# A pre-norm decoder layer: two quarters' attention outputs summed in PSUM, cross scores negated in the keys' norms, and the first cross rows requested beside their norms

## The chip, the core and the metric

The kernel runs on one core of one Trainium2 chip. The metric is device time in microseconds, the median over several runs. Engines are called TensorE (PE in the profile, with its weight loads as PEld), VectorE (DVE), ScalarE (ACT), GpSimd (POOL) and SyncE (SP). SP and POOL also issue DMAs, each from a queue of its own that is worked through in order.

## The reference

The layer takes `x` and a context `ctx_2048`, both (4, 512, 512) in float32, and adds three branches to `x`, each on layer-normalized rows.

```
q = (x @ Wq + bq).reshape(B, T, 128, 16)      # 16 heads, k and v likewise
y = softmax(q^T k / sqrt(128)) v              # attention over the 128 features of a head
x = x + y @ Wo + bo
# cross attention: norm(x) is (B, 512, 512); the 512 rows are split into 8 heads of 64
qk = einsum('bhdq,bhdl->bhql', norm(x), ctx) / sqrt(64)
x = x + gamma * einsum('bhql,bhdl->bhdq', softmax(qk), ctx)
# feed-forward with ternary weights, hidden size 1365
x = x + (silu(norm(x) w1q^T) * (norm(x) w3q^T)) w2q^T
```

`w1q`, `w3q`, `w2q` are weights rounded to -1, 0 or 1 times their mean absolute value.

## The kernel before

**Phase A (0 to about 285 us).** For each of four batches the normalized rows become a Gram matrix (`gram_upper`, `gram_rest`); `keys_of` multiplies it by the key weights, `scores` forms the scores and their softmax, and the result is turned and kept in device memory (`kept_e`). The steps run over four quarters j of the heads and, inside, over the four batches b. Beside it `kept_weights` splits the value and output weights into three parts (h, l, d) and stores them; `scale_steps` sums the absolute values of the feed-forward weights. Matrix products are made from halves in a 32-bit format that TensorE runs at one pass: an `h` and an `l` product into one PSUM bank, a `d` product into another, added by `total` (line 378).

**Side work.** Such work beside the main products is written as Python generators. A `Side` holds one: at each `tick` of the main products it takes as many steps as keep it in proportion (n steps in `of` ticks). `products` ticks three times for each pair of output blocks, six times in all (`PRODUCT = 6`): after the second k of the h and l matmuls, after their evictions, and at the end of the pair. A `yield` in a generator ends a step.

**The attention outputs (about 285 to 825 us).** A loop over b and j makes, for each quarter, `values_out` (the products pu, of the rows with the output weights: u), and `values_of` (the products pm, of u with the value weights: ms). Between pu and pm u has to be split in three parts: ScalarE makes uh (line 197), VectorE ul and ud (198, 199). `output(b, j, ...)` is one plain float32 matmul for each of four row groups (po, line 570; 512 columns, shown as two records) and an addition on VectorE into the accumulators `accs` (line 571); it is called after the *next* quarter's `values_out`, so that it lies between that quarter's pu and pm. After the last quarter the accumulators are stored as `x_a`. All weights come in through `weights`, 12 tiles of 256 KB for each product from a ring of 20, and the turned softmax by `turned_kept` (eT, a ring of two); both are issued on SP, where the order is the program's (`manual_schedule` for SP and GpSimd). On the other engines the order is made by a planner when the program is built, from its own costs and the program's order.

**Cross attention.** For batch b - 1 it starts in the outputs of batch b. `row_norms` (line 686) takes mean and variance of each accumulator row, a step for each row group, and turns them on their side through a small store (`norm_a`) and two loads (`norms`). `cross` (704) then works in 16 rounds of two softmax blocks: `fetch` loads 64 rows of `x_a` (xd) and of the context (kd), twice over the partitions; `split` makes q and the two halves of the keys, with the norms as ScalarE's and VectorE's operands; `softmax_rows` makes the scores (xs), their row maxima (line 755), a factor on these (756), the exponential (761) and the division by its sum; `transpose_rows` turns the result (xp). A round of four is a chunk: the context rows (`keys`, turned to `vals`, matmuls vt), the matmuls xo (794), and the addition of `gamma` times the result to the rows of `x_a` (`xc`, line 802), which is stored as `x_c`. All these DMAs are issued on GpSimd. `settle` (613) multiplies a column of a loaded tile by a one made from a fresh eviction on VectorE, so that VectorE, in its place in the order, takes the wait for the load.

The steps of `row_norms` and the first of `cross` (`AHEAD` of them, 17) are ticked as `aside` in the first 12 ticks after the output of a batch is finished (18 in batch 1); `begin_cross` then hands the 56 that remain to `side`, over 48 ticks (42 in batch 1). So the end of one batch's cross attention and the beginning of the next lie in the same product. Batch 3's cross attention runs beside the feed-forward of the first batches.

**Feed-forward (from about 825 us).** Products h (line 1183) and y (1221), with weights kept on the chip.

Five small things set the order where the change touches it. The eT ring has two tiles, the ms ring four and the accumulators' eight. PSUM has eight banks, shared by all products. The pool `c_x` has a single tile for each of xd, kd and `late` (keys and xc), so each of these loads waits until the tile before it has been read.

Of the kernel before, what the change touches and what calls it, by code (L numbers as in the profile page):

```python
# [11 lines left out]
F32 = mybir.dt.float32  # L12
# [7 lines left out]
P = 128  # L20
# [21 lines left out]
def decoder_layer_kernel(  # L42
# [161 lines left out]
    def load(dst, src):  # L204
        nc.sync.dma_start(dst, src)
        return dst
# [89 lines left out]
    def kept_weights(pool):  # L296

        def items():
            for j in range(HG):
                for k in range(KC):  # L300
                    yield "o", j, k, None
                for k in CHUNKS:
                    yield "v", j, k, None

        sources = {}

        def bring(n, j, k):
            if n == "o":
                t = pool.tile([P, GW], F32, tag="raw_v", bufs=4, name=f"o_raw_{j}_{k}")
                load(t, by_group(wo[j * T : (j + 1) * T, :], k))  # L310
                return t
            if k == KC - 1:
                sources[j] = raw_of("v", j, pool, load, 4)
            return sources[j][1](k)

        coming = []
        for item in itertools.chain(items(), [None, None]):
            if item is not None:
                coming.append((item[:3], bring(*item[:3])))
                if len(coming) < 3:  # L320
                    continue
            (n, j, k), t = coming.pop(0)
            gate = gates[0]
            if n == "v":
                fold(k, t, sources[j][0], gate)
            tri = Tri(
                *(pool.tile([P, GW], F32R, tag="made", bufs=4, name=f"{n}{p}_{j}_{k}") for p in "hl"),
                t.bitcast(F32R),
            )
            halves_of_weight(tri.h, tri.l, t, gate)  # L330
            third_of_weight(tri)
# [5 lines left out]
    KEPT_STEPS = 2 * 2 * HG * KC  # L337

    def weights(n, b, j, wp):

# [223 lines left out]
    def turned_kept(b, j):  # L564
        return load(ep.tile([P, GW], F32, tag="e", name=f"eT_{b}_{j}"), kept_e[b, j])

    def output(b, j, eT, ms, accs):
        for g in range(NG):
            po = bank(f"po_{b}_{j}_{g}")
            nc.tensor.matmul(po, lhsT=eT[:, ts(g, DH)], rhs=ms[g], start=True, stop=True)  # L570
            nc.vector.scalar_tensor_tensor(accs[g], po, S * S, accs[g], ALU.mult, ALU.add)
            if j == HG - 1:
                nc.gpsimd.dma_start(by_group(x_a[b], g), accs[g])
# [104 lines left out]


    xscale = 1.0 / math.sqrt(XD)  # L680
    CROSS_STEPS = 3 * 4 * NC + 14
    NORM_STEPS = 2 * NG + 3
    AHEAD = NORM_STEPS + 6
    norms = {}

    def row_norms(b, accs):


        mv = small.tile([P, NG, 2], F32, tag="mvc", bufs=2, name=f"mv_c_{b}")
        for g in range(NG):  # L690
            yield
            moments(mv[:, g, :], accs[g], f"c_{b}_{g}")
        rstd = rstd_of(mv, f"c_{b}")
        mean, var = (mv[:, :, i : i + 1].rearrange("p c s -> p (c s)") for i in range(2))
        nc.vector.tensor_scalar(mean, mean, -1.0, None, ALU.mult)
        nc.vector.tensor_copy(var, rstd)
        nc.gpsimd.dma_start(norm_a[b].rearrange("(p g) s -> p g s", g=NG), mv)
        norms[b] = small.tile([P, 2 * NC, 2], F32, tag="norms", bufs=2, name=f"norms_{b}")
        for half in (slice(0, XD), slice(XD, P)):
            nc.gpsimd.dma_start(norms[b][half], norm_a[b].rearrange("(n p) s -> p n s", p=XD))  # L700
        for _ in range(NG + 3):
            yield

    def cross(b, cx, cin, cpp, cpt):

# [6 lines left out]
        def load(dst, src):  # L712
            nc.gpsimd.dma_start(dst, src)  # L713
            return dst

        def late(name, src):
            return load(cx.tile([P, T], F32, tag="late", name=f"{name}_{b}"), src)

        def fetch(n):

# [22 lines left out]
        def softmax_rows(n, h):  # L743
# [8 lines left out]
                scs.append(sc)  # L752
            nmax = small.tile([P, 2], F32, tag="xnmax", name=f"xnmax_{b}_{n}_{h}")
            for i in range(2):
                nc.vector.reduce_max(nmax[:, i : i + 1], scs[i], axis=AX.X)  # L755
            nc.vector.tensor_scalar(nmax, nmax, -xscale, None, ALU.mult)
            den = small.tile([P, 2], F32, tag="xden", name=f"xden_{b}_{n}_{h}")
            ps = []
            for i in range(2):
                p = cpp.tile([P, T], F32, tag="p", name=f"p_{b}_{n}_{h}_{i}")  # L760
                nc.scalar.activation(  # L761
                    p,
                    scs[i],
                    AF.Exp,
                    bias=nmax[:, i : i + 1],
                    scale=xscale,
                    accum_out=den[:, i : i + 1],
                )
                ps.append(p)
# [13 lines left out]

        def turn_values(c):
            vals[c] = cin.tile([P, NC, P], F32, tag="vals", bufs=1, name=f"vals_{b}_{c}")
            transpose_blocks(vals[c], rows[c], f"vt_{b}_{c}", True)

        def weigh_values(c, xc):
            pt = [pts.pop(2 * c + j) for j in range(2)]
# [12 lines left out]
            nc.vector.scalar_tensor_tensor(y, po, gam, xc, ALU.mult, ALU.add)  # L802
            return lambda: load(x_c[b][ts(c, P), :], y)

        raw, halves, vals, pts, rows, ps = {}, {}, {}, {}, {}, {}
        fetch(0)
        yield
        yield
        settle(norms[b][:, 0, :])
        yield  # L810
        split(0)
        yield
        fetch(1)
# [4 lines left out]
        for i in range(len(order) + 3):  # L818
            c, phase = divmod(i, 4)
            if phase == 3 and c < NC:  # L820
                rows[c] = late(f"keys_{c}", kv[b][ts(c, P), :])
            if i < len(order):
                ps[order[i]] = softmax_rows(*order[i])
            if i < len(order):
                yield
            if phase == 2 and c > 0:
                store = weigh_values(c - 1, rows.pop(c - 1))
                yield
            if 2 <= i < len(order) + 2:
                n, h = order[i - 2]  # L830
                transpose_rows(n, h, ps.pop((n, h)))
            if i % 2 == 0 and i // 2 + 1 < heads:
                split(i // 2 + 1)
            if i % 2 == 0 and i // 2 + 2 < heads:
                fetch(i // 2 + 2)
            if phase == 2 and c > 0:
                store()
            if i < len(order) + 2:
                yield
            if phase == 0 and c > 0:  # L840
                turn_values(c - 1)
            if phase == 1 and c > 0:
                rows[c - 1] = late(f"xc_{c - 1}", x_a[b][ts(c - 1, P), :])
            if i < len(order) + 2:
                yield

# [189 lines left out]
    PRODUCT = 6  # L1036
    TICKS = 2 * HG * PRODUCT
    quant, aside, side = Side(), Side(), Side()
    waiting, accs = None, None

    def tick():
        quant.tick()
# [18 lines left out]

    for b in range(B):
        for j in range(HG):
            if b == 0 and j == 0:
                wo_tiles = weights("o", b, j, wp)
                accs = accumulators(0)
                load(bo_bc, bo.to_broadcast([P, D]))
            else:
                if j == HG - 1 and b + 1 < B:
                    next_accs = accumulators(b + 1)  # L1070
                wo_tiles = weights("o", b, j, wp)
            u3 = values_out(b, j, x3, wo_tiles, tick if b + j > 0 else turning())
            if b == 0 and j == 0:
                quant = Side(each(ternary_steps, stp), 2 * PIECES, B * TICKS - 2 * PRODUCT)
            if waiting:
                output(*waiting)
            if j == 0 and b > 0:
                aside.rest()
                crossing = itertools.chain(row_norms(b - 1, accs), cross(b - 1, *cpool))
                aside = Side(itertools.islice(crossing, AHEAD), AHEAD, (3 if b == 1 else 2) * PRODUCT)  # L1080
                accs = next_accs
            if j == 1 and b > 1:
                begin_cross(TICKS)
            if j == HG - 2:
# [30 lines left out]
    rows_next = rows_f(1)  # L1115
    for _ in ffn_0:
        pass
    output(*waiting)
    for _ in row_norms(B - 1, waiting[4]):
        pass  # L1120
    apools.close()

# [21 lines left out]
    crossing = itertools.chain([None] * 11, cross(B - 1, *cpool))  # L1144
    before = Side(itertools.chain(side.steps, [None] * LEFT), LEFT, 9)
    aside = Side(itertools.islice(crossing, AHEAD), AHEAD, 9)

# [9 lines left out]
        if at > 9:  # L1157
            last.tick()

    last = Side(crossing, CROSS_STEPS - 6, 2 * (NHC + NC) + 2 - 9)  # L1160
# [118 lines left out]
```

## Time and profile before

| | us |
|---|---|
| median of 3 runs | 1145.51 |
| lowest and highest | 1143.5, 1145.91 |
| the profiled execution | 1143.08 |
| span of that execution, first to last instruction | 1141.3 |
| TensorE busy | 1124.5 |
| VectorE busy | 808.1 |
| ScalarE busy | 562.4 |
| additions into acc, L571, 64 of 685 ns | 42.9 |
| output matmuls, L570, 128 records | 58.1 |
| row maxima of the cross scores, L755, 128 of 681 ns | 84.7 |
| their factor, L756, 64 of 186 ns | 11.9 |

The granted TensorE clock is 1.0 throughout. Busy times of an engine add up instructions and tell nothing of who waits; for that the profile has a view of waits (who waited, for whom, in how many places and how long) and a timeline. A matmul of 512 columns in the fast format shows 0.39 us, but the next one starts 0.227 us after it, and on VectorE a 512-column operation that shows 0.68 us lets the next start after 0.60 us: durations overlap their neighbours, and starts tell the pace. A `d` matmul of a product belongs to L368, an `h` to L356, an `l` to L357. The names pu, pm, po, xs, xp, xo and vt are those of the PSUM tiles.

### The profile page before, as it was taken

What the parts mean: (1) busy time and instruction counts of PE and PEld (TensorE: products, weight loads), DVE (VectorE), ACT (ScalarE), POOL (GpSimd) and SP (SyncE); (2) the same over time, 40 slices, a digit from 0 to 9 for tenths busy, and PEclk for the clock granted to TensorE, in tenths of its full rate; (3) what the DMA queues carried; (4) which work ended last, traced back from release to release, by engine and by line L of the source; (5) the groups of instructions that cost most, each with busy time, mean ns of one, the idle gap of its engine ahead of it and who ended that gap; (6) DMA issues with size and microseconds to landing.
All of it is one profiled execution on the core that took longest, in us unless ns stands there. A gap on an engine that the chain in (4) does not pass through costs nothing.

```text
span 1141.3 us, 16617 instructions
## 1 busy us (share of the span) xinstructions
PE 1124.5 (99%) x5406; PEld 874.1 (77%) x5406; DVE 808.1 (71%) x1616; ACT 562.4 (49%) x1200; POOL 204.1 (18%) x377
## 2 busy tenths in 40 slices
PE   9999999999999999999999999999999999999998
PEld 6778888888777777777767777577677877778886
DVE  7678676865556786898778788696887669537252
ACT  5375545553322334665646565465566557434020
POOL 2011001010111132232223213221222212000000
PEclk9999999999999999999999999999999999999999
DMA  9257879794999899978779977896941422121200
GB/s 308 80 177 242 277 251 327 241 326 149 386 351 384 302 316 332 332 231 299 240 221 333 319 235 255 252 332 224 328 152 65 148 65 65 47 74 37 93 1 37
DMA packets 145844, 252.04 MB, mean 221 GB/s; under 512 B 17032, under 2 KB 48008, under 8 KB 145758
## 3 DMA queue, kind: packets, MB, share of 16 engines
q1 hardware_dynamic: 124830, 187.48, 48.6%
q0 software_dynamic: 20928, 63.50, 17.4%
q8 instruction: 43, 0.70, 0.2%
q14 instruction: 43, 0.35, 0.1%
HBM read 196.37 MB, written 54.54 MB: 220 GB/s over the span
## 4 chain that ended last, share of the span: by engine, by line
PE 80%; DMA 7%; DVE 5%; issue 5%; ACT 2%; POOL 1%; SPq 0%; POOLq 0%; DVEq 0%; ACTq 0%
PE h L1183 13%; PE y L1221 7%; PE sc L529 5%; PE xo L794 4%; PE xp L128 4%; PE po L570 3%; PE xs L750 2%; PE xs L751 2%; DMA kd<-in_kv_dram 2%; PE pm_2d L368 1%; PE pu_0h L357 1%; PE pm_3h L356 1%; PE pu_3h L356 1%; PE pu_0d L368 1%; PE py_3h L356 1%
## 5 line engine op out<-in xcount | busy, mean ns | idle before, releaser
L1183 PE MATMUL h<-fxh,t 128*128 128x512 f32 (+1 forms) x352 | 139.8, 397 | 0.0
L1183 PE MATMUL h<-fxl,t 128*128 128x512 f32 (+1 forms) x352 | 137.5, 390 | 0.0
L761 ACT ACTIVATE p<-xs,xnmax 128x512 f32<-128x512 f32 x128 | 86.9, 686 | 94.9 <-PE xp L128 55.2
L755 DVE TENSOR_REDUCE xnmax<-xs 128x1 f32<-128x512 f32 x128 | 84.7, 681 | 2.8 <-PE xs L751 2.8
L1183 PEld LDWEIGHTS h<-fxh,t 128*128 128x128 f32 (+1 forms) x352 | 65.0, 185 | 16.4 <-issue 1.9
L1183 PEld LDWEIGHTS h<-fxl,t 128*128 128x128 f32 (+1 forms) x352 | 65.0, 185 | 14.6 <-DVE fxl L141 0.4
L1221 PE MATMUL y<-t,gh 128*128 128x512 f32 (+1 forms) x176 | 69.3, 394 | 0.0
L1221 PE MATMUL y<-t,gl 128*128 128x512 f32 (+1 forms) x176 | 68.8, 391 | 0.0
L128 PEld LDWEIGHTS xp<-ident,p 128*128 128x128 f32 x512 | 59.0, 140 | 11.2 <-issue 2.4
L131 ACT COPY pt<-xp 128x512 f32<-128x512 f32 x96 | 54.3, 590 | 26.5 <-PE xp L128 26.5
L128 PE MATMUL xp<-ident,p 128*128 128x128 f32 x512 | 66.4, 273 | 0.1
L713 POOL DMA_DIRECT2D xd<-x_a x64 | 33.7, 531 | 169.5 <-DVE qs L734 112.8
L1192 ACT ACTIVATE th<-h,scales_w 128x512 f32<-128x512 f32 (+1 forms) x44 | 30.4, 691 | 65.7 <-PE h L1183 65.5
L529 PE MATMUL sc<-y,q_raw 128*128 128x128 f32 x512 | 59.3, 275 | 0.0
L529 PEld LDWEIGHTS sc<-y,q_raw 128*128 128x128 f32 x512 | 58.4, 192 | 0.2
L570 PE MATMUL po<-m,eT 128*128 128x512 f32 x128 | 58.1, 595 | 0.4 <-DVE u L378 0.4
L794 PE MATMUL xo<-pt,vals 128*64 128x512 f32 x256 | 58.5, 598 | 0.0
L197 ACT ACTIVATE uh<-u 128x512 fp32r<-128x512 f32 x64 | 40.2, 632 | 28.2 <-DVE u L378 28.1
L750 PE MATMUL xs<-kh,qs 128*128 128x512 f32 x128 | 51.1, 400 | 2.1 <-DVE vals L802 1.4
L669 POOL DMA_DIRECT2D t_w<-tern_w x43 | 28.6, 666 | 125.1 <-DVE tern_w L661 117.7
L751 PE MATMUL xs<-kl,qs 128*128 128x512 f32 x128 | 50.1, 391 | 0.0
L773 ACT ACTIVATE p<-p,xrden 128x512 f32<-128x512 f32 x64 | 47.1, 736 | 4.3 <-DVE xrden L771 3.9
(243 smaller groups left out, 2841.4 us busy)
## 6 DMA issues: line engine op xcount, KB each, us to landing
oh<-kept_oh SPq DMA_DIRECT2D x64, 256.0 KB, 6.6
ol<-kept_ol SPq DMA_DIRECT2D x64, 256.0 KB, 7.2
od<-kept_od SPq DMA_DIRECT2D x64, 256.0 KB, 5.2
vh<-kept_vh SPq DMA_DIRECT2D x64, 256.0 KB, 6.4
vl<-kept_vl SPq DMA_DIRECT2D x64, 256.0 KB, 6.5
vd<-kept_vd SPq DMA_DIRECT2D x64, 256.0 KB, 4.6
xd<-x_a POOLq DMA_DIRECT2D x64, 128.0 KB, 5.5
kd<-in_kv_dram POOLq DMA_DIRECT2D x64, 128.0 KB, 6.1
```

The lines of the kernel that those rows point to most:

```text
L128: nc.tensor.transpose(pt[:, ts(k, P)], src[:, ts(k, P)], ident)
L131: nc.scalar.copy(dst, pv)
L529: nc.tensor.matmul(sc[:, ts(g, DH)], lhsT=w[k][:, ts(g, DH)], rhs=ys[k][:, ts(g, DH)], start=(k == 0), stop=(k == KC - 1),)
L570: nc.tensor.matmul(po, lhsT=eT[:, ts(g, DH)], rhs=ms[g], start=True, stop=True)
L750: nc.tensor.matmul(sc, lhsT=q[:, ts(m, P)], rhs=kh, start=True, stop=False)
L751: nc.tensor.matmul(sc, lhsT=q[:, ts(m, P)], rhs=kl, start=False, stop=True)
L755: nc.vector.reduce_max(nmax[:, i : i + 1], scs[i], axis=AX.X)
L761: nc.scalar.activation(p, scs[i], AF.Exp, bias=nmax[:, i : i + 1], scale=xscale, accum_out=den[:, i : i + 1],)
L773: nc.scalar.mul(ps[1], ps[1], rden[:, 1:2])
L794: nc.tensor.matmul(po[half, :], lhsT=vals[c][:, l, half], rhs=pt[j][:, l, :], start=(l == 0), stop=(l == NC - 1),)
L1183: nc.tensor.matmul(ph[:r, :], lhsT=t[:, block(i, k)], rhs=fxT[j][:, k, :], start=(k == 0 and j == 0), stop=(k == KC - 1 and j == 1),)
L1221: nc.tensor.matmul(py, lhsT=g[i][j][:r, ts(c, P)], rhs=t2[:r, i, :], start=(i == 0 and j == 0), stop=(i == NHC - 1 and j == 1),)
```

## The change

- `kept_weights` takes two empty steps after each of its first two loads; `KEPT_STEPS` grows from 64 to 68.
- `output` gets a pair of quarters: for each row group two matmuls accumulate in one PSUM bank, and one addition follows. It is called after `values_out` of quarter 2 (for quarters 0 and 1) and of quarter 0 of the next batch (for 2 and 3). The ms ring grows to eight tiles, the accumulators' falls to four; both eT tiles are held until the pair is used.
- The accumulators' four loads move to quarter 1 of their own batch, behind that quarter's output weights, and the load of `bo_bc` goes with them in batch 0; the bias is added after quarter 1's `values_of`.
- `row_norms` multiplies the inverse deviation by -1/8 where it copied it. The cross scores come out negated and scaled: the row maxima become minima, the factor on them is gone, and the exponential has a scale of -1.
- The first `fetch` is issued right after the small store `norm_a`; the loads of `norms` come three steps later; `settle` of the norms is gone. `AHEAD` falls from 17 to 14.
- The store of `x_c` moves to the beginning of the next round, behind the request for the next keys.

```diff
@@ kept_weights
                 if len(coming) < 3:
+                    yield
+                    yield
                     continue
...
-    def output(b, j, eT, ms, accs):
+    def output(b, j, pair, accs):
         for g in range(NG):
             po = bank(f"po_{b}_{j}_{g}")
-            nc.tensor.matmul(po, lhsT=eT[:, ts(g, DH)], rhs=ms[g], start=True, stop=True)
+            for i, (eT, ms) in enumerate(pair):
+                nc.tensor.matmul(
+                    po, lhsT=eT[:, ts(g, DH)], rhs=ms[g], start=(i == 0), stop=(i == 1)
+                )
             nc.vector.scalar_tensor_tensor(accs[g], po, S * S, accs[g], ALU.mult, ALU.add)
...
@@ row_norms
-        nc.vector.tensor_copy(var, rstd)
+        nc.vector.tensor_scalar(var, rstd, -xscale, None, ALU.mult)
         nc.gpsimd.dma_start(norm_a[b].rearrange("(p g) s -> p g s", g=NG), mv)
+        for _ in range(3):
+            yield
         norms[b] = small.tile([P, 2 * NC, 2], F32, tag="norms", bufs=2, name=f"norms_{b}")
         for half in (slice(0, XD), slice(XD, P)):
             nc.gpsimd.dma_start(norms[b][half], norm_a[b].rearrange("(n p) s -> p n s", p=XD))
-        for _ in range(NG + 3):
+        for _ in range(4):
             yield
...
@@ softmax_rows
-                nc.vector.reduce_max(nmax[:, i : i + 1], scs[i], axis=AX.X)
-            nc.vector.tensor_scalar(nmax, nmax, -xscale, None, ALU.mult)
+                nc.vector.tensor_reduce(nmax[:, i : i + 1], scs[i], axis=AX.X, op=ALU.min)
...
-                    scale=xscale,
+                    scale=-1.0,
...
@@ cross
-        fetch(0)
-        yield
-        yield
-        settle(norms[b][:, 0, :])
-        yield
+        if accs:
+            for at, _ in enumerate(row_norms(b, accs)):
+                if at == NG:
+                    fetch(0)
+                yield
+        else:
+            fetch(0)
+            yield
+            yield
+            yield
...
             if phase == 3 and c < NC:
-                rows[c] = late(f"keys_{c}", kv[b][ts(c, P), :])
+                keys_rows[c] = late("keys", c, kv[b])
+            if phase == 3 and c > 0:
+                store()
...
                 store = weigh_values(c - 1, rows.pop(c - 1))
+                if c == NC:
+                    store()
                 yield
...
-            if phase == 2 and c > 0:
-                store()
...
-    u3p, mp = apool("a_u3", 12), apool("a_m", 4)
-    accp, xnp = apool("a_acc", 8), apool("a_xn_kept", 4)
+    u3p, mp = apool("a_u3", 12), apool("a_m", 8)
+    accp, xnp = apool("a_acc", 4), apool("a_xn_kept", 4)
...
-            if b == 0 and j == 0:
-                wo_tiles = weights("o", b, j, wp)
-                accs = accumulators(0)
+            wo_tiles = weights("o", b, j, wp)
+            if j == 1:
+                accs = accumulators(b)
+            if b == 0 and j == 1:
                 load(bo_bc, bo.to_broadcast([P, D]))
-            else:
-                if j == HG - 1 and b + 1 < B:
-                    next_accs = accumulators(b + 1)
-                wo_tiles = weights("o", b, j, wp)
             u3 = values_out(b, j, x3, wo_tiles, tick if b + j > 0 else turning())
...
-            if waiting:
-                output(*waiting)
+            if len(waiting) == 2:
+                output(*at, waiting, accs)
+                waiting = []
...
-            if j == 0:
+            if j == 1:
                 biased(accs)
...
-            waiting = [b, j, eT, ms, accs]
+            waiting.append((eT, ms))
+            at = b, j
```

More of the change, by code (lines that the diff above doesn't have):

```diff
@@ L335, in kept_weights @@
             yield
-    KEPT_STEPS = 2 * 2 * HG * KC
+    KEPT_STEPS = 2 * 2 * HG * KC + 4
     def weights(n, b, j, wp):
@@ L680, in decoder_layer_kernel @@
     xscale = 1.0 / math.sqrt(XD)
-    CROSS_STEPS = 3 * 4 * NC + 14
-    NORM_STEPS = 2 * NG + 3
-    AHEAD = NORM_STEPS + 6
+    CROSS_STEPS = 3 * 4 * NC + 11
+    NORM_STEPS = NG + 7
+    AHEAD = NORM_STEPS + 3
     norms = {}
@@ L700, in row_norms, with cross @@
             nc.gpsimd.dma_start(norms[b][half], norm_a[b].rearrange("(n p) s -> p n s", p=XD))
-        for _ in range(NG + 3):
+        for _ in range(4):
             yield
-    def cross(b, cx, cin, cpp, cpt):
+    def cross(b, accs, cx, cin, cpp, cpt):
         def load(dst, src):
@@ L714, in load, with late @@
             return dst
-        def late(name, src):
-            return load(cx.tile([P, T], F32, tag="late", name=f"{name}_{b}"), src)
+        def late(name, c, src):
+            return load(cx.tile([P, T], F32, tag="late", name=f"{name}_{b}_{c}"), src[ts(c, P), :])
         def fetch(n):
@@ L785, in turn_values @@
             vals[c] = cin.tile([P, NC, P], F32, tag="vals", bufs=1, name=f"vals_{b}_{c}")
-            transpose_blocks(vals[c], rows[c], f"vt_{b}_{c}", True)
+            transpose_blocks(vals[c], keys_rows.pop(c), f"vt_{b}_{c}", True)
         def weigh_values(c, xc):
@@ L803, in weigh_values @@
             return lambda: load(x_c[b][ts(c, P), :], y)
-        raw, halves, vals, pts, rows, ps = {}, {}, {}, {}, {}, {}
-        fetch(0)
-        yield
-        yield
-        settle(norms[b][:, 0, :])
-        yield
+        raw, halves, vals, pts, rows, keys_rows, ps = {}, {}, {}, {}, {}, {}, {}
+        if accs:
[8 more added lines that the diff above has]
+            yield
         split(0)
@@ L842, in cross @@
             if phase == 1 and c > 0:
-                rows[c - 1] = late(f"xc_{c - 1}", x_a[b][ts(c - 1, P), :])
+                rows[c - 1] = late("xc", c - 1, x_a[b])
             if i < len(order) + 2:
@@ L1038, in decoder_layer_kernel @@
     quant, aside, side = Side(), Side(), Side()
-    waiting, accs = None, None
+    waiting = []
     def tick():
@@ L1074, in decoder_layer_kernel @@
                 quant = Side(each(ternary_steps, stp), 2 * PIECES, B * TICKS - 2 * PRODUCT)
-            if waiting:
-                output(*waiting)
+            if len(waiting) == 2:
+                output(*at, waiting, accs)
+                waiting = []
             if j == 0 and b > 0:
                 aside.rest()
-                crossing = itertools.chain(row_norms(b - 1, accs), cross(b - 1, *cpool))
+                crossing = cross(b - 1, accs, *cpool)
                 aside = Side(itertools.islice(crossing, AHEAD), AHEAD, (3 if b == 1 else 2) * PRODUCT)
-                accs = next_accs
             if j == 1 and b > 1:
@@ L1117, in decoder_layer_kernel @@
         pass
-    output(*waiting)
-    for _ in row_norms(B - 1, waiting[4]):
+    output(*at, waiting, accs)
+    for _ in row_norms(B - 1, accs):
         pass
@@ L1143, in decoder_layer_kernel @@
     LEFT = (NORM_STEPS + CROSS_STEPS - AHEAD) * 3 * PRODUCT // TICKS
-    crossing = itertools.chain([None] * 11, cross(B - 1, *cpool))
+    crossing = itertools.chain([None] * 8, cross(B - 1, None, *cpool))
     before = Side(itertools.chain(side.steps, [None] * LEFT), LEFT, 9)
@@ L1158, in tick @@
             last.tick()
-    last = Side(crossing, CROSS_STEPS - 6, 2 * (NHC + NC) + 2 - 9)
+    last = Side(crossing, CROSS_STEPS - 3, 2 * (NHC + NC) + 2 - 9)
     half_scale, both_scales = (scales[n][:, 0:1] for n in ("w1", "w3"))
```

## The prediction, made before the changed kernel was run

> **What bounds the kernel now.** I read the page first, for the load of each engine.
>
> ```profile
> span 1141.3 us, 16617 instructions
> ...
> PE 1124.5 (99%) x5406; PEld 874.1 (77%) x5406; DVE 808.1 (71%) x1616; ACT 562.4 (49%) x1200; POOL 204.1 (18%) x377
> ```
>
> TensorE is 99% busy, and the change takes no matmul away: 128 matmul records of L570 stay 128. So time can only come out of the places where TensorE stands still. The view of waits, kept to TensorE, lists them all (who waited, for whom, total us, times, longest):
>
> ```profile
> PE vt L128 <- DMA keys<-in_kv_dram: 2.9, 2, 1.8
> PE gt L475 <- ACT G L438: 2.0, 1, 2.0
> PE pu_1h L357 <- DMA ol<-kept_ol: 1.5, 1, 1.5
> PE pm_1h L356 <- ACT p L761: 1.5, 1, 1.5
> PE xs L750 <- DVE vals L802: 1.4, 1, 1.4
> PE idle L236 <- DVE sums_w L632: 1.1, 1, 1.1
> PE pu_2h L356 <- ACT pu_2t L363: 0.6, 1, 0.6
> PE xs L750 <- DVE m L378: 0.4, 1, 0.4
> PE po L570 <- DVE u L378: 0.4, 1, 0.4
> ...
> PE pm_2h L357 <- DVE ul L198: 0.3, 1, 0.3
> ```
>
> They sum to 12.7 us, of which 1.1 us (the start) can't be touched: about 11 us is the most that the change can win. Third, I took the timeline around each wait. For the keys of batch 2, on GpSimd's queue (start, length, engine, line, what, in brackets the idle time before and who ended it):
>
> ```profile
> 550.07 0.54 POOL L697 DMA_DIRECT2D norm_a<-mv_c  x1 [8.01 <-DVE mv_c L696]
> 552.02 1.40 POOL L700 DMA_DIRECT2D norms<-norm_a  x2 [1.41 <-DMA norm_a<-mv_c]
> 553.41 0.57 POOL L713 DMA_DIRECT2D xc<-x_a  x1
> ...
> 560.38 0.56 POOL L713 DMA_DIRECT2D x_c<-vals  x1 [5.65 <-ACT pt L131]
> 561.48 0.55 POOL L713 DMA_DIRECT2D keys<-in_kv_dram  x1
> ```
>
> The queue is in order. xc stands behind the norms that wait for their own store; the x_c store needs xc; the keys stand behind that store and leave at 561.5, so TensorE misses them by 1.8 us at 568. Fourth, VectorE's timeline just after the last matmul of pu_3 of batch 2 (648.0):
>
> ```profile
> 651.48 0.69 DVE L198 TENSOR_TENSOR ul<-u,uh 128x512 fp32r<-128x512 f32 x1
> 652.08 0.69 DVE L571 SCALAR_TENSOR_TENSOR acc<-po,acc 128x512 f32<-128x512 f32 x1
> 652.68 0.68 DVE L199 SCALAR_TENSOR_TENSOR ud<-uh,ul 128x512 fp32r<-128x512 f32 x1
> 653.28 0.69 DVE L571 SCALAR_TENSOR_TENSOR acc<-po,acc 128x512 f32<-128x512 f32 x1
> 653.88 0.68 DVE L198 TENSOR_TENSOR ul<-u,uh 128x512 fp32r<-128x512 f32 x1
> ```
>
> The last ul ends 6.6 us after pu's last matmul. Today the four output matmuls (3.43 us in the chain) stand between pu and pm, and TensorE does not notice. The additions start every 0.60 us, so that is what each costs VectorE.
>
> **Part by part.** A negative number is time saved.
>
> *(a) Staggered loads of kept weights.* At 76.7 ScalarE waits 1.96 us for o_raw, whose three loads were asked for in one tick; the evictions of gt queue behind it, and TensorE waits 2.0 us. With two empty steps after each of the first two loads, the first product is made in tick 5 and not in tick 1, after the evictions in tick 3. The cover for later work is loose: no other kept-weight row is in TensorE's list. Bounds -2.0 and 0; taken -1.9.
>
> *(b) Loads of acc and bo.* The five loads (256 KB each, one every 0.68 us on SP while DMA share is 1.05) leave the place ahead of quarter 0's v weights: 3.4 us of transfer. pu_1's ol came 1.5 us late, so -1.5 (bounds -1.5, 0). In later batches the four loads move from quarter 3 of the batch before, past five weight sets, to quarter 1. There they wait for the x_a stores and row statistics of the batch before, half a product old by then; the v weights behind them landed 6 us (batch 1) and 14 us (later) or more before their use (landings estimated from the bytes that the DMA records moved). 0.
>
> *(c) Two quarters in one sum.* TensorE: the same 64 matmuls, now 6.9 us in a block after pu of even quarters, none after odd. VectorE: 32 additions fewer at 0.60 us, 19 us; VectorE is at 71% and ends few waits, so that in itself is 0. What counts is where the block is gone: eight odd quarters, where pm now follows pu at once. Quarter 0 of batch 0 runs like that already: its last ul ends 3.8 us after pu, TensorE wants it 3.2 us after (14 matmuls at 0.227 us). Three quarters without cross work (1 and 3 of batch 0, 1 of batch 1) get that plus some ternary work: 0.5 us each, +1.5 (bounds +0.6, +4.2: with VectorE's other work in the gaps where the additions were). In quarter 3 of batch 1 to 3, cross matmuls after the second k of pm put the need off to 4.8, 5.1 and 5.3 us; the last ul came at 5.9, 6.6 and 6.2 us with two additions ahead of it, 1.2 us less without. ScalarE's last uh comes 0.4 us late in batch 1. Together +0.8 (0 to +3.5).
>
> *(d) The eT load on SP.* With both buffers held until the pair's sum, the third eT waits for the output block, and all weights behind it on SP wait too, about 7 us after even quarters. The next o weights have 10.9 us of pm to land and need 8 loads x 0.68 = 5.4 us; in batch 0 they landed 3 to 6 us early, later at least 4. Only quarter 1 of batch 0 is short: its v weights landed 5.1 us early, and pm now starts 3.4 + 1.5 us sooner. +0.8 (0 to +2.5).
>
> *(e) Cross start.* xd and kd (4 requests, 0.53 us each on GpSimd) leave before the norms, and the norms' requests come three steps later, when the store (4 KB, median 4.0 us to landing) is down. They now pass xc rather than block it. settle's two small VectorE operations (0.14 and 0.16 us) go; ScalarE waits for the norms itself, with the next softmax queued behind it. Steps on that side fall from 17 to 14 in the same ticks, and the 56 that follow stay. x_c's store moves behind the next keys' request on GpSimd: the values' buffer is wanted a step group later. Batch 2: the 1.8 us for keys goes; so does the 1.5 us for p at 589, where four acc additions (582.9 to 585.4) stood ahead of the scores' maxima. But 3.4 us of cover goes too; there the transfers were the late part (ScalarE stood 3.8 us for xd at 576.9): the first xd is asked for at about 553 and not 562, its split can run at its turn, near 564 and not 568.8, and the second request follows 5 us sooner. -2.9 (bounds -3.3, 0). Batch 3: waits of 1.0 and 1.4 us, but the keys are asked for only 1 us sooner and xd perhaps 3 us, against 3.4 us of cover gone: -1.5 (bounds -2.4, +2.5). Batch 1, quarter 2: waits of 0.6, 0.4, 0.4 and 0.3 us, behind ScalarE standing 5.6 us for xd; transfers and TensorE both move up by about 3 us. -0.3 (-1 to +1).
>
> The DMA share from 560 to 580 is 1.00. The Trainium skill, "DMA: Bandwidth & Descriptors", section "Issuing engines are not separate DMA queues", says that requests of all engines share the same 16 engines, so another issuing place buys little; by it the keys' 2.8 us would stay, and the sum be that much smaller. The row speaks for order, not bandwidth: GpSimd's queue stood 5.65 us with the keys unasked.
>
> *(f) Scores negated.* 64 operations of 0.19 us mean (L756) go from the path from maxima to Exp; the factor rides on a copy that exists four times. reduce as a minimum costs what L755's 681 ns is, or at worst the 684 ns of a full two-input pass. ScalarE waits 36.9 us for L756, hidden behind TensorE. 0, between -1 and +0.5.
>
> Sum: -1.9 - 1.5 + 1.5 + 0.8 + 0.8 - 2.9 - 1.5 - 0.3 = -5.0 us. The profiled execution took 1143.08 us (span 1141.3 and 1.8 around it), 2.4 us below the median of the runs, 1145.51; it becomes 1138.1, the median 1140.5.
>
> The Trainium skill, "Perfetto Trace Analysis", section "Identifying the Most-Contended Engine", calls matmul busy time a poor measure and takes weight-load busy time instead. By it, 77%, 267 us would be free and VectorE's 19 us might all come through; the gaps, 12.7 us, are what a change without matmuls taken away can reach here.
>
> **The rivals.** *Cover lost (slower).* Without the output block, pm waits for ul in every odd quarter. Price: 1.4 us at the three plain quarters, 1.1, 1.5 and 0.9 at the three quarters 3, 3.4 at quarters 1 of batch 2 and 3: 14.5 us, less (a), (b) and the keys' 2.8, 6.2 us: +8 us, 1153.5. It decides once the eight places lose over about 1 us each, the 8.1 us of gains by eight. For it: VectorE is 97 to 100% busy from 490 to 500 and 640 to 660. Against: quarter 0 of batch 0, and 1.2 us less work ahead of the last ul.
>
> *Order was not the cause (same).* Keys and xd land no sooner because DMA is full; only (a) and (b) come, -3.4, against +3.1 of (c) and (d): 1145.2. Against: DMA share is 0.8 to 0.9 over most of that stage.
>
> *All waits go (faster).* Cover holds and every wait named goes: -9.3, 1136.2. That VectorE's 19 us come through is excluded by TensorE's 99%.
>
> **Numbers.** A measurement of this kernel tells 0.2%, 2.3 us, from no change. My forecast 0.58, all waits gone 0.12, order not the cause 0.14, cover lost 0.16: faster 0.70, same 0.14, slower 0.16. The range runs from 1135, just past the best case, to 1148, a third of the way into the lost cover.
>
> **What would show it.** Additions to acc x32 and L756's row gone. TensorE's list without gt, pu_1h on ol and vt on keys; new short rows of pm on ul or uh, all under 1 us. On SP, eT waiting for po. If TensorE's waits sum to over 11 us, with pm in odd quarters ahead, the cover was worth more than I took; if xs or vt still wait for DMA, order was not the cause.

## The result and the profile after

The changed kernel takes 1156.37 us (median of 6 runs, 1152.92 to 1156.77); the kernel before took 1144.12 us (median of 6, 1141.95 to 1145.91). The ratio is 1.0098, with a 95% interval of [1.0079, 1.0117]: slower by about 11 us, where 1140.5 was forecast and the range ended at 1148. The profiled execution took 1156.47 us, its span 1154.7, 13.4 more than before.

The page of the changed kernel, span, load of the engines and granted clock in 40 slices:

```profile
span 1154.7 us, 16563 instructions
...
PE 1134.6 (98%) x5406; PEld 877.8 (76%) x5406; DVE 782.7 (68%) x1512; ACT 561.3 (49%) x1200; POOL 202.7 (18%) x377
...
PEclk9999999999999998999989999999999999999999
```

VectorE lost 25.4 us of work (808.1 to 782.7), as the edit says. TensorE has as many instructions as before and 10 us more busy time: two slices of the clock row show an 8. The waits of TensorE (for whom, total us, times, longest):

```profile
PE pm_1d L370 <- DMA vd<-kept_vd: 3.4, 3, 2.3
PE pm_1h L358 <- ACT uh L197: 2.4, 1, 2.4
PE pm_1h L359 <- DMA vl<-kept_vl: 2.2, 6, 0.7
PE pm_1h L359 <- DVE ul L198: 1.7, 3, 1.0
PE tot_w L649 <- ACT kh L277: 1.7, 1, 1.7
PE idle L236 <- DVE sums_w L637: 1.1, 1, 1.1
PE gt L477 <- ACT G L440: 0.9, 1, 0.9
PE pm_1h L358 <- DMA vh<-kept_vh: 0.9, 2, 0.5
PE sc L531 <- DVE y L380: 0.5, 1, 0.5
```

The rows shown of before for vt, xs, pm on p and pu_2 are gone. In their place stand pm_1 rows (quarter 1) on value weights (6.5 us) and on the split of u (4.1 us), and in phase A tot_w and sc. Both kernels have the same outputs behind them where pu_1 and pu_3 start, so these points can be set beside each other. The 13.4 us are then: phase A +2.2; from pu_1 to pu_3 of batch 0 +3.0, of batch 1 +6.1, of batch 2 +2.8, of batch 3 -1.7; all else +1.0. The waits of pm above lie at quarter 1 of these stretches. (Batch 3's gain is not the pairing's: in the run no_pair below, which does without it, that stretch is 3.1 us shorter than before.)

Batch 1, quarter 1: SyncE's queue (start, length, what it issues):

```profile
397.65 1.09 SPq L205 DMA_DIRECT2D vd<-kept_vd  x2
407.47 0.32 SPq L205 DMA_DIRECT2D eT<-kept_e  x1
407.84 0.44 SPq L205 DMA_DIRECT2D oh<-kept_oh  x1
...
414.46 1.75 SPq L205 DMA_DIRECT2D od<-kept_od  x4
418.68 1.96 SPq L205 DMA_DIRECT2D acc<-in_x_dram  x4
420.98 0.33 SPq L205 DMA_DIRECT2D vh<-kept_vh  x1
```

and in the kernel before:

```profile
396.39 0.42 SPq L205 DMA_DIRECT2D eT<-kept_e  x1
...
410.75 0.38 SPq L205 DMA_DIRECT2D vh<-kept_vh  x1
```

In the changed kernel the eT load stands 8.6 us for the output block; then eight output weights, their third parts and the four accumulators go out ahead of the first vh. Counted from the start of pu_1 (413.48 before, 419.02 now), eT is issued 11.5 us ahead of it and not 17.1, and vh 2.0 us behind it and not 2.7 ahead; TensorE could begin pm 11.3 us after that start and not 13.9, since no output block lies between. TensorE, and the clock in four stretches (columns: length, busy time and count by engine, then granted clock, DMA share and GB/s):

```profile
435.24 0.47 PE L359 MATMUL pm_1h<-ul,vl 128*128 128x512 f32 x1 [0.69 <-DMA vl<-kept_vl]
...
438.49 0.50 PE L370 MATMUL pm_1d<-ud,vd 128*128 128x512 f32 x1 [2.32 <-DMA vd<-kept_vd]
...
445.00 0.63 PE L358 MATMUL pm_1h<-uh,vh 128*128 128x512 f32 x1
445.42 0.63 PE L359 MATMUL pm_1h<-ul,vl 128*128 128x512 f32 x1
```

```profile
439.00:446.00 7.00, 6.41 (x16) 4.50 (x16) 1.85 (x3) 2.30 (x4) 0.00 (x0) 0.51 0.94 346
446.00:453.00 7.00, 7.00 (x33) 5.75 (x32) 3.48 (x7) 1.34 (x3) 3.40 (x6) 1.00 0.92 254
...
592.80:599.60 6.80, 6.29 (x14) 4.42 (x15) 5.50 (x10) 2.57 (x7) 3.93 (x7) 0.50 0.46 125
600.00:607.00 7.00, 7.00 (x33) 5.79 (x32) 4.12 (x8) 4.45 (x10) 0.08 (x1) 1.00 0.72 227
```

After the stands the granted clock is 0.5 for 6.83 us, twice (from 439.16 and 592.76): 16 and 14 matmuls in 7 us where 33 fit, a start every 0.427 us and not every 0.227. That is 16 x 0.2 = 3.2 us and 14 x 0.2 = 2.8 us, at most 6 of the 13.4 us, with no wait to show for it. In each stretch only 11 of these matmuls start after the last operand that came late (vd at 441.45, ul at 595.18); counting these alone, the estimate is 4.4 us.

Batch 2, quarter 1 is another case. VectorE's timeline, and the step of ScalarE that it waits for (in brackets the idle time before and who ended it):

```profile
588.27 0.72 ACT L740 ACTIVATE qs<-xd,norms 128x512 fp32r<-128x512 f32 x1 [6.42 <-DMA xd<-x_a]
...
589.02 0.75 DVE L741 SCALAR_TENSOR_TENSOR qs<-xd,norms,qs 64x512 fp32r<-64x512 f32 x1 [6.41 <-ACT qs L740]
589.81 1.48 DVE L380 SCALAR_TENSOR_TENSOR u<-pu_1t,pu_1d 128x512 f32<-128x512 f32 x2
591.20 0.48 DVE L665 TENSOR_SCALAR above_w<-tern_w,scales_w 128x512 bf16<-128x512 f32 x1
591.92 0.69 DVE L198 TENSOR_TENSOR ul<-u,uh 128x512 fp32r<-128x512 f32 x1 [0.23 <-ACT uh L197]
```

VectorE is not busy; it stands 6.41 us for qs, whose first half on ScalarE waits for a transfer of cross rows (xd), and the totals of u are queued behind it. So pm_1 stands 2.4 us for uh.

GpSimd's queue in batch 2, answering to the five lines of before:

```profile
560.99 0.54 POOL L702 DMA_DIRECT2D norm_a<-mv_c  x1 [8.67 <-DVE mv_c L701]
561.65 1.05 POOL L720 DMA_DIRECT2D xd<-x_a  x2
...
569.09 1.43 POOL L707 DMA_DIRECT2D norms<-norm_a  x2 [4.03 <-DMA norm_a<-mv_c]
570.51 0.58 POOL L720 DMA_DIRECT2D keys<-in_kv_dram  x1
```

The cross start does what was said: xd is asked for 0.66 us after the store began, and the keys 9.5 us after it (before 11.4); TensorE waits for them no more.

### The profile page after: what moved, and what is told of

Its sections match the earlier page's. It is cut to its first block, busy times and chain, and to the rows that moved or that the text cites. A ratio compares the mean times of both kernels' runs of the same rounds, so it can differ in the third digit from the quotient of the medians.

```text
span 1154.7 us, 16563 instructions
## 1 busy us (share of the span) xinstructions
PE 1134.6 (98%) x5406; PEld 877.8 (76%) x5406; DVE 782.7 (68%) x1512; ACT 561.3 (49%) x1200; POOL 202.7 (18%) x377
## 3 DMA queue, kind: packets, MB, share of 16 engines
q0 software_dynamic: 20928, 63.50, 17.1%
## 4 chain that ended last, share of the span: by engine, by line
PE 70%; issue 13%; DMA 10%; DVE 4%; POOL 1%; ACT 1%; SPq 0%; POOLq 0%; DVEq 0%; ACTq 0%
PE h L1194 13%; PE y L1232 7%; PE xp L128 4%; PE xo L800 4%; PE po L573 4%; PE xs L758 2%; PE xs L757 2%; PE sc L531 2%; DMA vh<-kept_vh 1%; PE pm_1d L370 1%; DMA kd<-in_kv_dram 1%; DMA vd<-kept_vd 1%; PE pm_3h L359 1%; PE pm_3h L358 1%; PE pm_2d L370 1%
## 5 line engine op out<-in xcount | busy, mean ns | idle before, releaser
L128 PEld LDWEIGHTS xp<-ident,p 128*128 128x128 f32 x512 | 59.2, 140 | 10.6 <-issue 2.4
```

What stands on the lines that cost most here:

```text
L128: nc.tensor.transpose(pt[:, ts(k, P)], src[:, ts(k, P)], ident)
```

## The experiments

Theories: **Q**, SyncE's queue brings the weights of quarter 1 late; **C**, the output block between pu and pm was cover, and TensorE now meets whatever is late; **R**, the cross start is the loss. "no_pair" and the like are the names of the runs.

**no_pair**: the changed kernel with an output and an addition for each quarter, the accumulators' loads and the rings as before; the rest of the change is kept.

```diff
-            if len(waiting) == 2:
-                output(*at, waiting, accs)
-                waiting = []
+            if waiting:
+                output(*waiting)
...
```

> The changed kernel with the pairing undone: one output, one addition and one acc load set for each quarter as before, rings as before; the staggered kept weights, the early cross rows and the negated scores stay. Theory Q (the pairing makes SP hold weights back) and theory C (the pairing takes the cover between pu and pm away) both expect nearly the whole loss gone: 1143 to 1147 us, with 2 us of phase A's loss still there. Rival R (the loss comes from the cross start) expects 1152 or more.

1138.14 us, 0.9951 [0.9933, 0.997]: faster than before by 5 us, and faster than expected. R falls. Without the pairing the rest is a gain; the pairing, with the later accumulator loads and the rings that belong to it, turns it into a loss of 11. Its clock is 1.0, and no wait of pm is over 0.3 us. Set beside this run, the profile of the changed kernel is 18.7 us longer, and 17.4 us of that lie between pu_1 and pu_3: 2.7, 7.3, 6.1 and 1.4 us in the four batches. From a pu_3 to the next pu_1 it is 0.2 to 0.4 us each.

**pair_only**: the kernel before with the pairing (its rings and its place of the accumulators' loads included), and with nothing else of the change.

> The kernel before with the pairing alone. Q and C expect the loss of quarters 1 of batches 0 and 1 (about 10 us) without phase A's 2 us: 1153 to 1158 us. R expects 1146 or less.

1163.07 us, 1.0166 [1.0142, 1.0191]: +19 us, more than either theory said. Pairing loses by itself. Its longest stand, 5.6 us of xs for the addition of the cross result in batch 2, is one that the changed kernel doesn't have, so the 19 us are not all of the kind that the changed kernel lost.

**eT4** (four eT tiles, so that no eT load waits for the block), **acc_early** (the accumulators' loads where they were, eight tiles), and both together. The first two lines are eT4's, the last acc_early's:

```diff
+    etp = apool("a_eT", 4)
-        return load(ep.tile([P, GW], F32, tag="e", ...), kept_e[b, j])
+        return load(etp.tile([P, GW], F32, tag="eT", ...), kept_e[b, j])
...
-            if j == 1:
-                accs = accumulators(b)
+                if j == HG - 1 and b + 1 < B:
+                    next_accs = accumulators(b + 1)
```

> The changed kernel with a ring of four for eT, taken from unused space, so that SP's eT load no longer waits for the output block. Q expects the 8.6 us stand of SP to go, and with it most of the late v weights in quarter 1 of batch 1, the 0.5 clock there, and a part in batch 0: 1147 to 1151 us. C expects at most 1 us: 1155 to 1157.

> The changed kernel with the four acc loads (and bo's) back in their old place and eight acc tiles. Q expects the 2.7 us that they take ahead of the v weights to go, but SP's stand to remain: 1151 to 1154 us. C expects 1156.

> The changed kernel with both of the repairs of SyncE's queue: four eT tiles, so that no eT load waits for the output block, and the loads of the accumulators in the place that they had before. Theory Q (what is left of the loss are late weights and the half clock behind them): the 2.1 us that vd still cost with the early accumulators go, and the 1.7 us of half clock with them, 1146 to 1148. Theory C (cover): TensorE then waits for ul, ud and uh instead, 1149 to 1151, no better than with the early accumulators alone. If the feed-forward stands 4 us for t as it did with four eT tiles alone, either is 5 us more, and the trace shows it.

eT4: 1154.42 us, 1.0087 [1.0067, 1.0108], by its time not to be told from the changed kernel. Two things cancel in it. From pu_1 to pu_3 its profile is 2.8 us shorter than the changed kernel's in batch 0 and 4.4 us in batch 1, where Q expected it, and no pm of batch 1 waits for a weight. But behind the last pu_3 it is 5.4 us longer, with a new stand in the feed-forward and 3.41 us of half clock from 838.28:

```profile
PE h L1195 <- DMA t<-t_w: 4.0, 1, 4.0
```

The load of this ternary tile is asked for late, since SyncE stands 9.5 us for the last output block: a by-product of this repair. So the time of eT4 does not decide between Q and C.

acc_early: 1150.5, 1.0053 [1.0037, 1.0069]: about 5 us won, a little more than Q expected, and against C's 1156. Late weights are a part of the loss.

Both: 1150.19, 1.0054 [1.0037, 1.0071], as acc_early alone and inside C's range. But this profile too has the new stand, 3.1 us, and takes 3.8 us more behind the last pu_3 than acc_early's. With the 5 us that the expectation adds in that case, the time lies below both ranges and nearer to Q's, so it does not decide either. What decides is the waits: no pm waits for a weight any more, and 4.9 us of waits for ul and ud are left. In quarter 1 of batch 1 the wait has only changed its name. TensorE's waits from 400 to 450 us with both repairs:

```profile
PE pm_1d L370 <- DVE ud L199: 1.9, 1, 1.9
PE pm_1h L359 <- DVE ul L198: 0.8, 1, 0.8
```

and VectorE's timeline in that quarter:

```profile
430.53 0.68 DVE L198 TENSOR_TENSOR ul<-u,uh 128x512 fp32r<-128x512 f32 x1
434.40 0.49 DVE L665 TENSOR_SCALAR above_w<-tern_w,scales_w 128x512 bf16<-128x512 f32 x1 [3.19 <-DMA tern_w<-in_w3t_dram]
434.81 0.69 DVE L199 SCALAR_TENSOR_TENSOR ud<-uh,ul 128x512 fp32r<-128x512 f32 x1
```

In the kernel before, the same ternary step stands for its load too, but behind all four ud and the additions:

```profile
433.97 0.49 DVE L660 TENSOR_SCALAR above_w<-tern_w,scales_w 128x512 bf16<-128x512 f32 x1 [3.33 <-DMA tern_w<-in_w3t_dram]
```

Now it lies ahead of the last ul and the last two ud.

**cover_back**: the kernel with both repairs, and with useless work in the place of the block.

```diff
+            elif j == 1 and b in (1, 2):
+                eT, ms = waiting[0]
+                for g in range(NG):
+                    nc.tensor.matmul(bank(f"cover_{b}_{g}"), lhsT=eT[:, ts(g, DH)], rhs=ms[g], ...)
```

> The changed kernel with both repairs of SyncE's queue (1150.2 us, 1.0054 of the kernel before) and, at quarter 1 of batches 1 and 2, four plain float32 matmuls between pu and pm whose result nobody reads: 6.9 us of useless work on TensorE where the output block stood. Theory C (cover, and the half clock that follows a stand): the waits for ul and ud there (1.9 + 0.8 us in batch 1, 0.2 + 1.3 in batch 2) and 1.6 us of half clock in each go, 7.4 us in all, so the time stays where it is: 1148.5 to 1151.5. Theory Q or any other in which TensorE had no need of cover: 6.9 us more, 1156 to 1157.5.

1150.7 us, 1.0054 [1.0034, 1.0073], the ratio of the kernel without this work: 6.9 us more work on TensorE (6.1 us by the starts of pm) cost nothing that shows outside an interval of about 2 us. Its matmuls in batch 1, and the waits from 400 to 450 us:

```profile
430.02 3.59 PE L1095 MATMUL cover<-m,eT 128*128 128x512 f32 x8
433.05 0.79 PE L358 MATMUL pm_1h<-uh,vh 128*128 128x512 f32 x1
```

```profile
PE pm_1h L359 <- DVE ul L198: 1.6, 1, 1.6
```

In both quarters pm starts 3.0 and 3.1 us later than without the dummy matmuls, and the next pu 3.0 and 3.7 us sooner relative to that: all paid back, the half clock behind the stands included (1.0 there now). Against the second profile of the same kernel (eT4_acc_early_again below), whose batch 2 has no half clock, 1.0 us of the 6.1 is not paid back. This shows theory C for these two quarters: an output block between pu and pm cost next to nothing there, because the time it took was otherwise lost.

**tern_later**: the kernel with both repairs, and no ternary step during quarter 1 of batch 1; the steps are spread over 12 ticks fewer, so their pace changes a little in all other quarters. **eT4_acc_early_again** is the same kernel without this edit.

```diff
-        quant.tick()
+        if not hold[0]:
+            quant.tick()
...
+            hold[0] = b == 1 and j == 1
...
-                quant = Side(each(ternary_steps, stp), 2 * PIECES, B * TICKS - 2 * PRODUCT)
+                quant = Side(each(ternary_steps, stp), 2 * PIECES, B * TICKS - 4 * PRODUCT)
```

> The changed kernel with both repairs of SyncE's queue, and no step of the ternary weights during the products of quarter 1 of batch 1 (they are made before and after). In the run without this VectorE stood 3.2 us there for the load of a ternary piece, with ud and ul of the last u behind it, and TensorE waited 1.9 + 0.8 us and then ran 3.4 us at half clock. Theory O (order: what is late is an operation of other work that waits for its own load in front of ul and ud, since no output block pays for its time): TensorE's waits in that quarter fall under 0.5 us, no half clock follows, and the time falls by 3 to 4.4 us against the same kernel without the edit (1150.2 us): 1146 to 1147.5. Theory P (pace: ul and ud are late since VectorE needs 0.60 us for each and pm comes at once): the waits stay over 1.5 us and the time within 1 us of 1150.

> The changed kernel with both repairs of SyncE's queue once more, beside the kernel without ternary steps in quarter 1 of batch 1, on the same chip: 1149 to 1151.5 by every theory.

1150.23 us, 1.0055 [1.0033, 1.0076], against 1150.85, 1.0054 [1.0035, 1.0074]: no difference, against O's expectation for the time. In that quarter O is right: the waits for ud and ul (2.6 + 0.8 us without the edit) and the half clock are gone, and the next pu starts about 5.5 us sooner. But then pu_2 waits, and quarter 2 takes 2.6 us longer. Waits of the run from 400 to 460 us:

```profile
PE pu_2h L358 <- ACT p L767: 1.4, 1, 1.4
PE pu_2h L358 <- ACT pu_2t L365: 1.0, 1, 1.0
```

The rest went in other places of the profile (batch 0's quarter 1 with 6.83 us of half clock, pm_3 1.9 us). So what stands ahead of ul on VectorE is the cause of that wait, but taking one away doesn't move the time of this kernel. Why the other places took back as much is left open: the changed pace of the ternary steps is one candidate, and scatter another, since the profiled execution took 1154.22 us, 4 us over its median.

**pair_23**: pairs of quarters 2 and 3 alone, on the kernel before with the early cross rows.

> The kernel before with the early cross rows (1135.7 us), and quarters 2 and 3 of each batch summed in PSUM; quarters 0 and 1 keep their own outputs, and the accumulators' loads their place. Theory (the loss of pairing sits at quarter 1, where pm follows pu without cover and the weights are short; quarter 3 lost only 0.2 to 0.5 us each in every traced run with pairs): 1135.5 to 1138. Rival (each pair costs about the same, 18 us over eight pairs): 1143 to 1146.

1140.01 us, 0.9957 [0.9943, 0.9971], against 0.9928 for the same without pairs: +3.3 us for four pairs, where pairing all cost 17 (no_pair to the changed kernel). It is over the theory's range by 2 us, and far below the rival's. Most of the loss belongs to quarter 1, as the stretches under no_pair say too. Of what this run lost, its profile puts 2.6 us behind the last pu_3.

**The other edits alone.** stagger_only: the stagger on the kernel before. cross_only: the early cross rows on it, scores not negated. no_pair_no_stagger: the same with negated scores.

> The kernel before with the staggered loads of the kept weights alone. The prediction said -1.9 us: 1141.5 to 1142.5. Rival: the wait of 2 us at gt shrinks, but new waits at tot_w and sc, about 2.5 us, take its place and more: 1144.5 to 1147.

> The kernel before with the early cross rows alone (first rows asked for beside their norms, x_c stores behind the next keys), scores not negated. Theory (order of GpSimd's queue is what counts, the factor on the maxima lies beside TensorE): within 1 us of the same with negated scores, 1135 to 1137. Rival (the factor stood on the path from maxima to exponential): 1139 to 1142.

> The kernel before with the early cross rows and the negated scores only: one output and one addition per quarter, loads of kept weights not staggered. In the run with single outputs and the stagger (1138.1 us, 5.2 below the kernel before) phase A ended about 2.4 us later than in the kernel before. Theory (the stagger costs what phase A loses): 1135 to 1136.5 us. Rival (the 2.4 us are made up behind phase A, since the stagger gives its 2 us at gt): 1138 to 1140.

stagger_only: 1145.88 us, 1.001 [0.9997, 1.0022], no gain. Waits up to 290 us:

```profile
PE gt L477 <- ACT G L440: 1.1, 1, 1.1
...
PE tot_w L646 <- ACT kh L277: 0.9, 1, 0.9
PE sc L531 <- DVE y L380: 0.8, 1, 0.8
```

gt fell from 2.0 to 1.1, and two waits that were not there took 1.7, as the rival said. cross_only: 1135.72 us, 0.9928 [0.9913, 0.9943]: -8 us. no_pair_no_stagger: 1136.56, 0.9935 [0.9919, 0.9951]: the negation makes no difference that can be seen. Its ratio is 1.6 thousandths under that of no_pair, which has the stagger in addition; the intervals overlap.

**cross_acc0** moves batch 0's accumulators and bo behind quarter 1's output weights, on cross_only; **cross_acc0_stag1** adds one empty step after each of the first two kept-weight loads.

```diff
+            if b == 0 and j == 1:
+                waiting[4] = accs = accumulators(0)
+                load(bo_bc, bo.to_broadcast([P, D]))
```

> The kernel before with the early cross rows (1135.7 us), and batch 0's accumulator loads and the load of bo behind quarter 1's output weights, ahead of its value weights; outputs as before. It is the prediction's term (b) by itself: the wait of pu_1 for the output weights (2.4 us in that profile, with 1.7 us of half clock behind it) goes, 1132.5 to 1134.5. Rival (the five loads, 3.4 us of transfer, hold the value weights of quarter 1 back instead): 1135.5 to 1138.

> The same with the loads of the kept weights staggered by one empty step, not two. Theory (any stagger turns the wait at gt into waits at tot_w and sc): 0.5 to 2 us above the same without stagger. Rival (half the stagger is enough for gt, and later work stays covered): 1 to 2 us below it.

1135.28 us, 0.9912 [0.9892, 0.9932], and 1134.33, 0.991 [0.9888, 0.9931]. These are the two lowest ratios, both faster than the kernel before by about 10 us; neither can be told from cross_only by its interval, so neither run decides between its two expectations. In the first profile pu_1's wait for ol falls from 2.4 to 0.6 us.

## Why the prediction was wrong, by its steps

**(c), cover: the step that failed, and (b) and (d) with it.** (c) took +2.3 us for the odd quarters, (d) +0.8 for the eT loads, and (b) nothing for the accumulators' loads in batches 1 to 3: 3.1 us for the pairing, which cost about 17. With both repairs of SyncE's queue, where no pm waits for a weight, the stretches from pu_1 to pu_3 still take 7.7 us more than in no_pair (5.2 in the second profile): that is about what cover was worth by itself, the half clock behind such waits included. The rest of the 17.4 us, by difference, came with late weights. Three things were wrong in (c). It priced quarter 1 of batches 2 and 3 at nothing by themselves and put them into (e). It took VectorE's pace (0.60 us an operation) as the limit for ul, where VectorE in fact stood for other work: 6.41 us for qs, 3.19 us for a ternary load. The trace of before had those stands already (3.33 us for the ternary load, 3.8 us for xd on ScalarE); the question that was missing is what stands on VectorE's list between the last total of u and the last ul once the additions are gone. And quarter 0 of batch 0, its evidence against the rival, runs without cross work beside it, so it was no sample of the rest.

**(b) and (d), SyncE's queue, priced apart.** (b) gave the later accumulator loads 0 in batches 1 to 3, because the value weights landed 6 us early; (d) let the eT load wait 7 us and held only quarter 1 of batch 0 short. Both delays are in one queue, ahead of the same weights: counted from pu_1 of batch 1, vh is issued 4.7 us later and could be used 2.6 us sooner, 7.3 us against the 6 that (b) had as slack. Putting the accumulators back won 5 us. Freeing the eT loads took 7.3 us off the stretches from pu_1 to pu_3 of batches 0 and 1 (eT4), well over (d)'s +0.8 and its bound of 2.5. The two gains do not add: over all four batches these stretches are about 10 us shorter with acc_early (in a profile 3.3 us under that run's median), 7.3 with eT4 and 9.7 with both. It was the sum of the two delays that went past the slack. In batch 0, (b) was right about ol (1.5 us before, 0.2 after), but its five loads then stood ahead of quarter 1's vh, and pm_1 waited 2.0 us for value weights there.

**Half clock.** No term had it. The prediction took the sum of waits as the whole of what TensorE can lose; 4.4 to 6 us of the loss have no wait at all.

**(a), the stagger.** -1.9 forecast; -0.3 to +2.2 thousandths alone, so a gain of 1.9 us is excluded. "No other kept-weight row is in TensorE's list" was the faulty reason: a list of waits shows what was late, not how little was to spare. ScalarE stood 3.62 us for a store of kept weights near 135 us before, 7.43 after.

**(e), the cross start: right, and too small.** -4.7 forecast for the three batches; cross_only shows -8 with an interval of about 1.7 us on either side, and the reason (order of GpSimd's queue, not bandwidth) held: rows of vt on keys went from 2.9 us to none. The forecast had charged it with cover that this experiment keeps, so the two numbers are not of the same thing.

**(f)**: 0 forecast, none to be seen.

The rival "cover lost" gave 1153.5 and was the nearest to the result. Its test, TensorE's waits over 11 us with pm in odd quarters ahead, is met: the waits sum to 15.8 us, 10.6 of them at pm_1. But it said that pm would wait for ul in every odd quarter; 6.5 of the 10.6 us are for value weights, and no pm_3 stands in the list, though it had 3.5 us for the three of them. That its number came near is partly luck. It got 0.16, mainly because the case against it rested on the one quarter that was unlike the others.

## What to carry to other kernels

Work that stands between a product and its consumer is not paid for by its own length: before taking it away, list for each engine what is queued ahead of the consumer's operands, and what each of these waits for. Delays in one in-order queue add up; price all edits that pass through it together, against the slack of the last thing behind them. Split such a change: the early cross rows alone were worth 8 us, and the part that saved VectorE 19 us of idle capacity lost 17. And read a repair by stretches as well as by its time: eT4 mended one place and broke another, and its time showed neither.

## What the runs showed of the hardware

The granted clock falls to 0.5 after stands that are short. Inside the runs every such stretch lasted 3.41 us or 6.83 us, and the stands of TensorE around their starts were as short as 0.5 + 0.9 us (cover_back at 318 us), 1.0 + 0.6 us (acc_early at 317 us), and 2.3 us (no_pair_no_stagger at 79 us). Length alone doesn't decide: stands of 2.9 us (cover_back at 833 us) and 3.0 us (tern_later at 836 us) passed at full clock, and at gt 2.1 us was followed by half clock in pair_23 while 2.2 us was not in pair_only. The Trainium skill, "TensorE: Matmul & The Clock Gate", section "HAM oscillation — how this bites in real kernels", asks for no gap over about 3.4 us; the length of the stretches agrees with such a window, but the gaps here that were followed by half clock were mostly well below it, and several together in a few microseconds were enough.
